# A transformer layer on one core: value projections grouped first, context steps queued behind units, and a layer norm cut into steps

## The chip, the core and the metric

The kernel runs on one core of one Trainium2 chip. The metric is the device time of one execution in microseconds (us), the median of three runs. TensorE (PE) multiplies matrices, VectorE (DVE), ScalarE (ACT) and GpSimd (POOL) work on vectors, and SyncE (SP) issues most of the DMA transfers. Each engine runs its own queue of instructions in order, and waits for other engines by semaphores.

## The reference

One post-norm decoder layer in float32, for x of 8 sequences of 100 tokens by 1024, and a context of 8 sequences of 722 tokens by 1024:

```
x = layernorm(x + retention(x))          # 8 heads, keys 128, values 256, gate; output projection Wo
x = layernorm(x + attention(x, context)) # 16 query heads, 4 key/value heads of 128
x = layernorm(x + ffn(x))                # silu(x w_gate) * (x w_up), then w_down, hidden 4096
```

The second line is where the change lies. Queries, keys and values of the tokens are q = x wq, k = x wk, v = x wv; q and k are RMS-normed and rotated. Keys and values of the context (k_ctx = context wk_ctx, normed, and v_ctx = context wv_ctx) are put in front of the tokens' own, and softmax(q k) v is projected by wo. The layer norm has no weights: (x - mean) / sqrt(var + eps).

## The kernel before

Everything is kept transposed, features on the 128 partitions and tokens in the columns, in two **halves** of four sequences (N = 400 columns). Products that are to have float32 accuracy are made of three matmuls on rounded parts: high by high (L90), high by low (L93), low by high (L94). The parts come from a *split* (L68): ACT casts to the rounded type, DVE subtracts to get the rest. A **unit** is one output block of 128 features for one half: 8 blocks of k by 3 matmuls, 24 matmuls of 128x400, in one PSUM bank (`proj`). PSUM has three banks for accumulators ("a"), four others ("s"), and one ("v"). Weights are loaded in pieces of 512 KB into `wst` (3 buffers, L74), and split into `w` (4 buffers). Context weights were split once at the start, and are loaded as 1 MB straight into a `w` buffer (`load_ws`, L84, from `wcd`).

The order of the program's text is mostly the order of each queue, but a scheduler may move instructions: `pin` keeps one in its place, `tc.high_priority()` pulls instructions ahead, `tc.issue_after(i)` queues one behind another without a wait.

The stages that the change touches, in order of time:

- **First output projection and layer norm** ("ln1", 500 to 611 us of the span). `out_proj(half, ...)` makes the 8 blocks m of one half, each from 16 blocks of k (two weights of 512 KB), adds the residual (`rs`, L271 or L269) into y, and sums the rows (L295). The norm of a half is done while the next matmuls run: the function returns a dictionary `todo` of what the next stage has to call before its k-th matmul group (`between`). Half 0's norm (`whole`: mean L320, y less mean L322, squares L301 and their sums L306, variance L324, scaling L312, split into z, store into zd) is called at once in the first block of half 1. Half 1's norm is partly early (`norm_early`, mean of seven blocks, L335, L337, L301) and ends in the next stage (`norm_late`, L291, L346, L343, L348, then L127 to L135, L312 and the z splits).
- **Second projections** ("l2", 587 to 850). z1[0] and z1[1] are the normed halves. For each of four key/value heads there are six weights: four of queries (i = 0 to 3), one of keys (4), one of values (5). They are taken in groups: (0..3) and (4, 5) for head 0, (0, 1), (2, 3), (4, 5) for the others; in a group all its weights run on z1[0], then on z1[1]. A query or key unit is followed by work on all other engines: square (L691, ACT), sum over partitions (L140, POOL), rotation (L148, L149 on ACT, L150 to L152 on DVE), inverse root (L127 to L135), scaling (L696), split (L68) and store into qd or kd. A value unit is copied to `vt` (L160, ACT), turned by four PE transposes (L163), split into vs (L687, one buffer) and stored into vd (L688).
- **The first context** is read by `load_context(0)`, called ahead of the second group: eight loads into `cs` (L634) and eight splits into the "big" tiles. The keys of the first two context products are made between groups: `context_keys` (L638) loads a key weight, and its `step` (L647) runs one more unit on the context, 24 matmuls of 128x362 or 128x360.
- **Second output projection and layer norm** ("lnp2", 1640 to 1750), the same `out_proj`, with one y buffer instead of two. Behind it come the feed-forward units; the first runs on z2[0] and carries the end of half 1's norm, and the next need half 1 as f and z.

The lines that order the second projections before the change:

```
for kv in range(NKV):
    for i0, i1 in ((0, 4), (4, 6)) if kv == 0 else ((0, 2), (2, 4), (4, 6)):
        if (kv, i0) == (0, 4):
            load_context(0)
        ws = [ws2.pop() if ws2 else load_w(w2[kv, i]) for i in range(i0, i1)]
        if (kv, i0) in ((1, 2), (2, 2)):
            step, kept = context_keys(kv - 1)
        if (kv, i0) in ((1, 2), (2, 0), (2, 2), (3, 0)):
            step(i0 == 0)
```

Of the kernel before, what the change touches and what calls it, by code (L numbers as in the profile page):

```python
# [16 lines left out]
P = 128  # L17
B, T, D = 8, 100, 1024
NB = 4
# [21 lines left out]
def decoder_layer(ctx, tc, xT, cT, w1, wo1, w2, wo2, wc, w3, wd, gw, qw, kw, trig, dec, mask, out):  # L41
# [12 lines left out]
    def bank(tag):  # L54
        return ps.tile([P, 512], F32, tag=tag, name=tag, bufs=banks[tag])

    def f32(ap):
        return ap.bitcast(F32)
# [4 lines left out]
    def split(dst, src):  # L63

        return split2(dst[:, 0], dst[:, 1], src)
# [4 lines left out]
    def load_w(src, w=None, pinned=None):  # L70
        st = wp.tile([P, KT * P], F32, tag="wst", name="wst", bufs=3)
        if w is None:
            w = wp.tile([P, 2, KT * P], FR, tag="w", name="w", bufs=4)
        nc.sync.dma_start(out=st, in_=src)  # L74
        if pinned:
            with tc.issue_after(pinned[0].ins), tc.issue_after(pinned[1].ins):
                split(w, st)
        else:
            split(w, st)
        return w  # L80
# [151 lines left out]
        return dcy  # L232


    def out_proj(half, w, load_o, res, yp, ybufs, p, make_z, dst, z, todo=None):


        og = load_o(half)
        y = None
        s1 = p.tile([P, N], F32, tag="s1", name="s1", bufs=2)  # L240
        early = {}
        first = 4 if half == 0 else 1
        for ms in [range(first)] + [[m] for m in range(first, KT)]:
            accs = [bank(("aaasaaaa", "sssaaass")[half][m])[:, :N] for m in ms]
            if half == 1 and KT - 1 in ms:
                todo = {QT: lambda: early.update(norm_early(y, s1, p))}
            for c in range(2):
                for m, acc in zip(ms, accs):
                    if half == 1 and m < 3:
                        with tc.high_priority():  # L250
                            wt = load_w(w[m, c])
                    else:
                        wt = load_w(w[m, c])
                    for k in range(KT):
                        kt = c * KT + k
                        pinned = between(todo, k) if c == 0 and m == ms[0] else False
                        rh, rl = og(kt)
                        a = acc if len(rh.shape) == 2 else bt(acc)
                        mmw(a, wt, k, rh, rl, kt == 0, kt == 2 * KT - 1, pinned)
            todo = None  # L260
            if y is None:
                y = yp.tile([P, KT, N], F32, tag="y", name="y", bufs=ybufs)
            for m, acc in zip(ms, accs):
                rs = yp.tile([P, N], F32, tag="rs", name="rs", bufs=2)
                nc.sync.dma_start(out=rs, in_=res[half, :, m])
                if early:
                    nc.vector.tensor_tensor(rs, rs, early["mean"], ALU.subtract)
                    with tc.high_priority():
                        nc.vector.tensor_tensor(y[:, m], acc, rs, ALU.add)  # L269
                else:  # L270
                    nc.vector.tensor_tensor(y[:, m], acc, rs, ALU.add)  # L271
                    add_up(s1, y, m)

        def whole():
            z.append(make_z(half))
            scaled(y, norm_root(y, s1, p), lambda m: dst[half, :, m], z[half])

        def late():
            norm_late(y, early, p)
            z.append(make_z(half))  # L280
            scaled(y, inv_root(p, early["vs"], eps_ln), lambda m: dst[half, :, m], z[half])

        if half == 0:
            return {QT: whole}, y
        sq = squares(y, p, [KT - 1])
        return {QT: lambda: summed(early["delta"], y[:, KT - 1], True, True),
                KT - 1: lambda: (summed(early["var"], early["sq"], True), summed(early["var"], sq, False, True), late())}, y
# [6 lines left out]
        if m > 0:  # L294
            nc.vector.tensor_tensor(s1, y[:, 0] if m == 1 else s1, y[:, m], ALU.add)  # L295

    def squares(y, p, ms):
        s2 = None
        for m in ms:
            sq = p.tile([P, y.shape[2]], F32, tag="sq", name="sq", bufs=2)  # L300
            nc.scalar.activation(sq, y[:, m], AF.Square)  # L301
            if s2 is None:
                s2 = sq
            else:
                s3 = p.tile([P, y.shape[2]], F32, tag="s2", name="s2", bufs=2)
                nc.vector.tensor_tensor(s3, s2, sq, ALU.add)  # L306
                s2 = s3
        return s2

    def scaled(y, r, dst, z=None):  # L310
        for m in range(KT):
            nc.vector.scalar_tensor_tensor(y[:, m], y[:, m], -0.5, r, ALU.mult, ALU.mult)  # L312
            if z is not None:
                split(z[m // QT][:, :, m % QT], y[:, m])
            nc.sync.dma_start(out=dst(m), in_=y[:, m])
# [294 lines left out]
    z1p = z1pool.__enter__()  # L610

    with sbuf("ln1", 1) as p:
        z1, todo = [], None
        for half in range(2):
            todo, _ = out_proj(half, wo1, load_o1, xT, p, 2, p, lambda _: [
                z1p.tile([P, 2, QT, N], FR, tag="z", name="z") for _ in range(2)], zd, z1, todo)
        ws2 = [load_w(w2[0, 0])]
        acc2 = [proj(ws2[0], z1[0], todo=todo)]


# [1 line left out]
    ka = kapool.__enter__()  # L622
    cz = []

    def load_context(b):

        cz.clear()
        for hf in range(2):
            n = SN[hf]
            z = [big([P, 2, QT, SH]) for _ in range(2)]  # L630
            for k in range(0, KT, 2):
                cs = wp.tile([P, KT * P], F32, tag="wst", name="cs", bufs=3)
                cs = cs[:, :2 * n].rearrange("p (k n) -> p k n", k=2)
                nc.sync.dma_start(out=cs, in_=cT[b, :, k:k + 2, hf * SH:hf * SH + n])  # L634
                split(z[k // QT][:, :, k % QT:k % QT + 2, :n], cs)
            cz.append(z)

    def context_keys(kv):  # L638

# [25 lines left out]
        return vt  # L665


    early = []
    with sbuf("l2", 2) as p:
        for kv in range(NKV):  # L670
            for i0, i1 in ((0, 4), (4, 6)) if kv == 0 else ((0, 2), (2, 4), (4, 6)):
                if (kv, i0) == (0, 4):
                    load_context(0)
                ws = [ws2.pop() if ws2 else load_w(w2[kv, i]) for i in range(i0, i1)]
                if (kv, i0) in ((1, 2), (2, 2)):
                    step, kept = context_keys(kv - 1)
                    early.append(kept)
                if (kv, i0) in ((1, 2), (2, 0), (2, 2), (3, 0)):
                    step(i0 == 0)
                for half in range(2):  # L680
                    bs = slice(half * NB, (half + 1) * NB)
                    for i in range(i0, i1):
                        acc = acc2.pop() if acc2 else proj(ws[i - i0], z1[half])
                        if i == 5:
                            tr = tokens_first(p, acc).rearrange("p (b d) -> p b d", b=NB)
                            vs = p.tile([T, NB, 2, P], FR, tag="vs", name="vs", bufs=1)
                            split2(vs[:, :, 0], vs[:, :, 1], tr)  # L687
                            nc.sync.dma_start(out=f32(vd[kv, :, bs]), in_=f32(vs))  # L688
                            continue
                        sq = p.tile([P, N], F32, tag="sq", name="sq")  # L690
                        nc.scalar.activation(sq, acc, AF.Square)  # L691
                        ss = all_red(p, sq, "ss")
                        tb = tq if i < 4 else tk
                        t = rope(p, acc, tb[:, 0], tb[:, 1], swapped=bank("s")[:, :N])
                        r = inv_root(p, ss, eps_k, at=bank("s")[:, :N])
                        nc.vector.scalar_tensor_tensor(  # L696
                            t, t, -0.5 if i < 4 else -0.5 * math.sqrt(P), r, ALU.mult, ALU.mult)
                        d = p.tile([P, NB, 2, T], FR, tag="d", name="d", bufs=3)
                        split2(d[:, :, 0], d[:, :, 1], bt(t))
                        nc.sync.dma_start(out=f32(qd[kv, i, :, bs] if i < 4 else kd[kv, :, bs]), in_=f32(d))  # L700
    z1pool.__exit__(None, None, None)


# [155 lines left out]


    with sbuf("lnp2", 1) as p:
        z2, todo = [], None
        for half in range(2):
            todo, y = out_proj(half, wo2, load_o2, zd, y2p, 1, p, make_z2, zd2, z2, todo)
        w0 = load_w(w3[0, 0])
        acc3 = [proj(w0, z2[0], tag=acc_tag(), todo=todo)]
        mixed2(y)
# [337 lines left out]
```

## Time and profile before

| | us |
|---|---|
| median of three runs | 2504.05 (2503.03 to 2505.15) |
| the profiled execution | 2504.06 |
| its span | 2502.3 |
| PE busy | 2463.2 |
| DVE busy | 1954.5 |
| ACT busy | 1343.0 |
| POOL busy | 464.8 |

The profile is of one execution. "Span" runs from the first to the last instruction; 1.76 us lie around it. Times in the text are us from the span's start. In a row of the profile, `L90 PE MATMUL a<-z,w` is the instruction of line 90 on PE that writes a tile named a from tiles z and w. A matmul's own duration (0.34 us) is longer than the distance to the next (0.181), since they overlap. "Granted clock" is the share of PE's full clock that was granted. DMA rows are transfers, and SPq rows are the issues of transfers on SP.

### The profile page before, as it was taken

Reading aid. Unit: us, or ns where it says so; the run is one execution under the profiler, and the core shown is the slowest. Engines: PE = TensorE matmul, PEld = TensorE weight load, DVE = VectorE, ACT = ScalarE, POOL = GpSimd, SP = SyncE. Lnnn points to the kernel's source line nnn. Section 1 sums busy time; section 2 is a strip of 40 time slices with the busy share of each in tenths; the row PEclk is TensorE's granted clock in tenths of the full one; section 3 lists DMA queues with packets and bytes.
Section 4 is the critical chain, followed back from the end, with each engine's and each line's share of the span. In section 5 each row is a group of like instructions: output and inputs, shape, how many; then the busy total and the mean of one; then the engine's idle time right before and its main releaser. Section 6 shows DMA issues by size and latency. Waiting matters only on the chain.

```text
span 2502.3 us, 37231 instructions
## 1 busy us (share of the span) xinstructions
PE 2463.2 (98%) x14068; PEld 2440.7 (98%) x14068; DVE 1954.5 (78%) x3101; ACT 1343.0 (54%) x2260; POOL 464.8 (19%) x234
## 2 busy tenths in 40 slices
PE   9999999997999999999999999999999999999997
PEld 9999999997999999999999999999999999999997
DVE  7778877567877688989999999866987777666756
ACT  6666676335767555656566666533544544432221
POOL 0111111002455343433433434100000000000000
PEclk9999999998999999999999999999999999999999
DMA  7333445774444654554554553574445444389731
GB/s 242 111 111 128 137 144 178 242 271 134 166 145 137 210 174 160 163 167 155 167 176 142 168 195 127 199 256 153 143 175 195 169 166 168 124 285 324 276 103 53
DMA packets 224451, 433.98 MB, mean 173 GB/s; under 512 B 47338, under 2 KB 168042, under 8 KB 211854
## 3 DMA queue, kind: packets, MB, share of 16 engines
q1 hardware_dynamic: 222542, 426.87, 50.2%
q0 software_dynamic: 1152, 4.19, 1.1%
q8 instruction: 111, 1.82, 0.3%
q14 instruction: 70, 0.57, 0.1%
q10 hardware_dynamic: 576, 0.52, 0.1%
HBM read 322.18 MB, written 109.35 MB: 172 GB/s over the span
## 4 chain that ended last, share of the span: by engine, by line
PE 93%; DVE 3%; DMA 2%; ACT 1%; issue 1%; POOL 0%; SPq 0%; DVEq 0%; ACTq 0%
PE a L94 20%; PE a L90 20%; PE a L93 20%; PE s L94 9%; PE s L93 9%; PE s L90 9%; PE v L94 2%; PE v L90 2%; PE v L93 2%; PE s L531 1%; PE s L734 1%; PE s L163 1%; DVE w L68 1%; DMA big<-o1d 1%; DVE y L312 0%
## 5 line engine op out<-in xcount | busy, mean ns | idle before, releaser
L90 PE MATMUL a<-big,w 128*128 128x400 f32 (+2 forms) x1808 | 609.5, 338 | 2.8 <-DMA w<-wcd 1.0
L93 PE MATMUL a<-big,w 128*128 128x400 f32 (+2 forms) x1808 | 609.3, 337 | 0.3 <-DVE big L68 0.3
L94 PE MATMUL a<-big,w 128*128 128x400 f32 (+2 forms) x1808 | 607.6, 337 | 0.4 <-DVE w L68 0.4
L68 ACT CAST w<-wst 128x1024 fp32r<-128x1024 f32 (+1 forms) x231 | 239.6, 1039 | 397.4 <-PE a L94 144.0
L68 DVE TENSOR_TENSOR w<-wst,w 128x1024 fp32r<-128x1024 f32 (+1 forms) x231 | 284.6, 1232 | 143.0 <-ACT w L68 141.7
L90 PEld LDWEIGHTS a<-big,w 128*128 128x128 f32 x1808 | 339.7, 188 | 5.9 <-ACT big L68 1.7
L93 PEld LDWEIGHTS a<-big,w 128*128 128x128 f32 x1808 | 340.3, 188 | 1.9 <-DVE big L68 1.0
L94 PEld LDWEIGHTS a<-big,w 128*128 128x128 f32 x1808 | 340.2, 188 | 1.2 <-DVE w L68 0.6
L90 PE MATMUL a<-z,w 128*128 128x400 f32 x680 | 236.4, 348 | 17.7 <-DVE t L150 16.0
L94 PE MATMUL a<-z,w 128*128 128x400 f32 x680 | 236.1, 348 | 0.0
L93 PE MATMUL a<-z,w 128*128 128x400 f32 x680 | 236.0, 347 | 0.0
L90 PE MATMUL s<-big,w 128*128 128x400 f32 x664 | 231.7, 349 | 2.4 <-ACT w L68 1.8
L94 PE MATMUL s<-big,w 128*128 128x400 f32 x664 | 229.9, 347 | 1.0 <-DVE w L68 1.0
L93 PE MATMUL s<-big,w 128*128 128x400 f32 x664 | 229.8, 346 | 0.0
L140 POOL PARTITION_ALL_REDUCE ss<-sq x56 | 150.7, 2693 | 328.8 <-DMA zd<-y 167.8
L651 POOL PARTITION_ALL_REDUCE kss<-ksq x64 | 166.7, 2604 | 127.8 <-ACT ksq L650 127.2
L90 PEld LDWEIGHTS a<-z,w 128*128 128x128 f32 x680 | 128.7, 189 | 19.5 <-DVE t L150 13.3
L768 ACT ACTIVATE s<-s,rk 128x400 f32<-128x400 f32 x160 | 87.9, 592 | 95.4 <-DVE sm L788 65.4
L90 PEld LDWEIGHTS s<-big,w 128*128 128x128 f32 x664 | 125.0, 188 | 5.3 <-ACT w L68 3.0
L94 PEld LDWEIGHTS a<-z,w 128*128 128x128 f32 x680 | 129.4, 190 | 0.0
L93 PEld LDWEIGHTS a<-z,w 128*128 128x128 f32 x680 | 128.7, 189 | 0.5
L94 PEld LDWEIGHTS s<-big,w 128*128 128x128 f32 x664 | 125.7, 189 | 1.7 <-DVE w L68 1.7
(356 smaller groups left out, 5443.8 us busy)
## 6 DMA issues: line engine op xcount, KB each, us to landing
wst<-in_w SPq DMA_DIRECT2D x135, 512.0 KB
w<-wcd SPq DMA_DIRECT2D x64, 1024.0 KB
wst<-in_wo SPq DMA_DIRECT2D x64, 512.0 KB
hd<-h SPq DMA_DIRECT2D x12, 1400.0 KB
wst<-in_wd SPq DMA_DIRECT2D x64, 256.0 KB
big<-o1d SPq DMA_DIRECT2D x16, 800.0 KB
qd<-d SPq DMA_DIRECT2D x32, 400.0 KB
q<-qd SPq DMA_DIRECT2D x32, 400.0 KB
```

The source lines that it names most:

```text
L68: return nc.scalar.copy(hi, src), nc.vector.tensor_tensor(lo, src, f32(hi), ALU.subtract)
L90: i = nc.tensor.matmul(acc, lh, rh, start=start, stop=False, skip_group_check=chain)
L93: nc.tensor.matmul(acc, lh, rl, start=False, stop=False, skip_group_check=chain)
L94: nc.tensor.matmul(acc, ll, rh, start=False, stop=stop, skip_group_check=chain)
L140: nc.gpsimd.partition_all_reduce(y, x, P, op)
L163: nc.tensor.transpose(tr[0:T, b * P:(b + 1) * P], vt[:, b * T:(b + 1) * T], ident)
L531: nc.tensor.matmul(bt(o)[:, b], vv[:, b * P:(b + 1) * P], pf[:, b], start=True, stop=True)
L651: nc.gpsimd.partition_all_reduce(ss[:, at], sq[:, at], P, RED.add)
L734: nc.tensor.transpose(tr[0:rows, (c - c0) * P:(c - c0 + 1) * P], vt[:, c * P:c * P + rows], ident)
L768: nc.scalar.activation(sc, sp, AF.Copy, scale=rk[:, c:c + 1])
```

## The change

Three things are done.

**Second projections.** The groups are now: the values of all four heads first, then for each head (0, 1) and (2, 3, 4). The first weight loaded is that of head 0's values. Context steps of keys come ahead of groups 2, 3, 5 and 7.

**The first context's steps.** `load_context` becomes a generator, `context_steps`; one of its eight load-and-split steps is taken ahead of each of the units 4 to 11, into buffers of its own (two), and both halves of its split are queued behind the split of the unit before (`tc.issue_after`).

**The norm of half 0.** In both output projections it is called in four steps: mean in block m = 0 of half 1, y less mean and squares of the first four blocks in m = 1, of the last four in m = 2, variance and the rest in m = 4. The inverse root reads the variance from PSUM without a copy. The weights of the first three blocks of half 1 are no longer loaded at high priority.

```diff
@@ out_proj
-            if half == 1 and KT - 1 in ms:
+            todo = steps.get(ms[0])
+            if half == 1 and KT - 1 in ms:
...
-                    if half == 1 and m < 3:
-                        with tc.high_priority():
-                            wt = load_w(w[m, c])
-                    else:
-                        wt = load_w(w[m, c])
+                    wt = load_w(w[m, c])
...
+        def centre():
+            kept["mean"] = bank("s")[:, :N]
+            pin(nc.tensor.matmul(kept["mean"], onem, s1, start=True, stop=True))
+        def less(ms):
+            for m in ms:
+                nc.vector.tensor_tensor(y[:, m], y[:, m], kept["mean"], ALU.subtract)
+            kept["sq"] = squares(y, p, ms, kept.get("sq"))
         def whole():
+            var = bank("v")[:, :N]
+            pin(nc.tensor.matmul(var, onem, kept["sq"], start=True, stop=True))
             z.append(make_z(half))
-            scaled(y, norm_root(y, s1, p), lambda m: dst[half, :, m], z[half])
+            scaled(y, inv_root(p, var, eps_ln), lambda m: dst[half, :, m], z[half])
...
-            return {QT: whole}, y
+            return {0: {QT: centre}, 1: {QT: lambda: less(range(QT))}, 2: {QT: lambda: less(range(QT, KT))},
+                    4: {QT: whole}}, y
@@ context_steps
-                cs = wp.tile([P, KT * P], F32, tag="wst", name="cs", bufs=3)
+                cs = pool.tile([P, KT * P if behind is None else 2 * SH], F32, tag="wst", name="cs", bufs=bufs)
...
-                split(z[k // QT][:, :, k % QT:k % QT + 2, :n], cs)
+                if behind is None:
+                    split(to, cs)
+                else:
+                    with tc.issue_after(behind[0].ins), tc.issue_after(behind[1].ins):
+                        split(to, cs)
...
+                yield
@@ second projections
+    groups = [[(kv, 5) for kv in range(NKV)]]
+    for kv in range(NKV):
+        groups += [[(kv, i) for i in range(2)], [(kv, i) for i in range(2, 5)]]
...
+        ctx0 = context_steps(0, p, 2, behind)
+        for g, group in enumerate(groups):
+            ws = [ws2.pop() if ws2 else load_w(w2[kv, i]) for kv, i in group]
+            if g in (2, 5):
+                step, kept = context_keys(len(early))
+                early.append(kept)
+            if g in (2, 3, 5, 7):
+                step(g in (3, 7))
...
+                    if 4 <= unit < 12:
+                        next(ctx0)
+                    acc = acc2.pop() if acc2 else proj(w, z1[half])
+                    unit += 1
...
+                        behind[:] = split2(vs[:, :, 0], vs[:, :, 1], tr)
...
+                    behind[:] = split2(d[:, :, 0], d[:, :, 1], bt(t))
```

More of the change, by code (lines that the diff above doesn't have):

```diff
@@ L232, in load_constants, with out_proj @@
         return dcy
-    def out_proj(half, w, load_o, res, yp, ybufs, p, make_z, dst, z, todo=None):
+    def out_proj(half, w, load_o, res, yp, ybufs, p, make_z, dst, z, steps={}):
         og = load_o(half)
@@ L259, in out_proj @@
                         mmw(a, wt, k, rh, rl, kt == 0, kt == 2 * KT - 1, pinned)
-            todo = None
             if y is None:
@@ L272, in out_proj @@
                     add_up(s1, y, m)
+        kept = {}
+        def centre():
[5 more added lines that the diff above has]
+            kept["sq"] = squares(y, p, ms, kept.get("sq"))
         def whole():
+            var = bank("v")[:, :N]
+            pin(nc.tensor.matmul(var, onem, kept["sq"], start=True, stop=True))
             z.append(make_z(half))
-            scaled(y, norm_root(y, s1, p), lambda m: dst[half, :, m], z[half])
+            scaled(y, inv_root(p, var, eps_ln), lambda m: dst[half, :, m], z[half])
         def late():
@@ L295, in add_up, with squares @@
             nc.vector.tensor_tensor(s1, y[:, 0] if m == 1 else s1, y[:, m], ALU.add)
-    def squares(y, p, ms):
-        s2 = None
+    def squares(y, p, ms, s2=None):
         for m in ms:
@@ L612, in decoder_layer @@
     with sbuf("ln1", 1) as p:
-        z1, todo = [], None
+        z1, todo = [], {}
         for half in range(2):
@@ L616, in decoder_layer @@
                 z1p.tile([P, 2, QT, N], FR, tag="z", name="z") for _ in range(2)], zd, z1, todo)
-        ws2 = [load_w(w2[0, 0])]
+        ws2 = [load_w(w2[0, 5])]
         acc2 = [proj(ws2[0], z1[0], todo=todo)]
@@ L623, in decoder_layer, with context_steps @@
     cz = []
-    def load_context(b):
+    def context_steps(b, pool, bufs, behind=None):
         cz.clear()
@@ L631, in load_context @@
             for k in range(0, KT, 2):
-                cs = wp.tile([P, KT * P], F32, tag="wst", name="cs", bufs=3)
+                cs = pool.tile([P, KT * P if behind is None else 2 * SH], F32, tag="wst", name="cs", bufs=bufs)
                 cs = cs[:, :2 * n].rearrange("p (k n) -> p k n", k=2)
                 nc.sync.dma_start(out=cs, in_=cT[b, :, k:k + 2, hf * SH:hf * SH + n])
-                split(z[k // QT][:, :, k % QT:k % QT + 2, :n], cs)
-            cz.append(z)
+                to = z[k // QT][:, :, k % QT:k % QT + 2, :n]
+                if behind is None:
[3 more added lines that the diff above has]
+                        split(to, cs)
+                if k == 0:
+                    cz.append(z)
+                yield
+    def load_context(b):
+        for _ in context_steps(b, wp, 3):
+            pass
     def context_keys(kv):
@@ L668, in decoder_layer @@
     early = []
-    with sbuf("l2", 2) as p:
[L670 to L700, printed above, removed]
@@ new lines, in decoder_layer @@
+    behind = [None, None]
+    groups = [[(kv, 5) for kv in range(NKV)]]
+    for kv in range(NKV):
+        groups += [[(kv, i) for i in range(2)], [(kv, i) for i in range(2, 5)]]
+    unit = 0
+    with sbuf("l2", 2) as p:
+        ctx0 = context_steps(0, p, 2, behind)
[6 more added lines that the diff above has]
+                step(g in (3, 7))
+            for half in range(2):
+                bs = slice(half * NB, (half + 1) * NB)
+                for (kv, i), w in zip(group, ws):
+                    if 4 <= unit < 12:
+                        next(ctx0)
+                    acc = acc2.pop() if acc2 else proj(w, z1[half])
+                    unit += 1
+                    if i == 5:
+                        tr = tokens_first(p, acc).rearrange("p (b d) -> p b d", b=NB)
+                        vs = p.tile([T, NB, 2, P], FR, tag="vs", name="vs", bufs=1)
+                        behind[:] = split2(vs[:, :, 0], vs[:, :, 1], tr)
+                        nc.sync.dma_start(out=f32(vd[kv, :, bs]), in_=f32(vs))
+                        continue
+                    sq = p.tile([P, N], F32, tag="sq", name="sq")
+                    nc.scalar.activation(sq, acc, AF.Square)
+                    ss = all_red(p, sq, "ss")
+                    tb = tq if i < 4 else tk
+                    t = rope(p, acc, tb[:, 0], tb[:, 1], swapped=bank("s")[:, :N])
+                    r = inv_root(p, ss, eps_k, at=bank("s")[:, :N])
+                    nc.vector.scalar_tensor_tensor(
+                        t, t, -0.5 if i < 4 else -0.5 * math.sqrt(P), r, ALU.mult, ALU.mult)
+                    d = p.tile([P, NB, 2, T], FR, tag="d", name="d", bufs=3)
+                    behind[:] = split2(d[:, :, 0], d[:, :, 1], bt(t))
+                    nc.sync.dma_start(out=f32(qd[kv, i, :, bs] if i < 4 else kd[kv, :, bs]), in_=f32(d))
@@ L861, in decoder_layer @@
     with sbuf("lnp2", 1) as p:
-        z2, todo = [], None
+        z2, todo = [], {}
         for half in range(2):
```

## The prediction

> **What bounds the kernel now.** I read the busy shares first, then PE's row of the 40 slices, then the waits of PE, then the stretches around each wait, two microseconds at a time.
>
> ```profile
> PE 2463.2 (98%) x14068; PEld 2440.7 (98%) x14068; DVE 1954.5 (78%) x3101; ACT 1343.0 (54%) x2260; POOL 464.8 (19%) x234
> ...
> PE   9999999997999999999999999999999999999997
> ```
>
> PE is busy for 98% of the span. So the end is the number of matmuls times their spacing, plus PE's holes and the slow clock behind them. The spacing is 0.181 us, 0.183 to 0.185 in the second half, so a unit of 24 matmuls lasts 4.36 to 4.4 us. Only one slice dips before the end, the tenth, and the waits of PE say who makes it:
>
> ```profile
> PE a L90 <- DVE t L150: 16.0, 2, 13.0
> PE s L90 <- ACT w L68: 1.8, 1, 1.8
> PE a L90 <- ACT d L68: 1.2, 1, 1.2
> ...
> PE a L90 <- DMA w<-wcd: 1.0, 2, 0.6
> ```
>
> (us in total, times, longest.) The first and third fall between 598 and 636 us, the second at 1663, the last at 678 and 740. The stretches add the clock after a stall (PE's busy time with its matmuls, granted clock third from the end):
>
> ```profile
> 598.00:612.00 14.00, 0.98 (x5) 0.65 (x4) 13.93 (x27) 8.05 (x16) 3.71 (x1) 0.65 0.69 246
> 612.00:614.00 2.00, 2.00 (x7) 1.98 (x7) 0.67 (x2) 0.39 (x1) 2.00 (x2) 0.50 0.00 0
> 614.00:616.00 2.00, 2.00 (x8) 1.98 (x7) 0.00 (x0) 1.93 (x5) 2.00 (x1) 0.54 0.00 0
> ...
> 636.00:638.00 2.00, 2.00 (x8) 1.97 (x8) 2.00 (x5) 1.89 (x5) 1.69 (x1) 0.58 0.95 371
> 638.00:640.00 2.00, 2.00 (x8) 1.97 (x8) 2.00 (x3) 0.68 (x2) 1.10 (x1) 0.56 0.37 143
> ...
> 1664.00:1666.00 2.00, 2.00 (x8) 2.00 (x7) 1.79 (x4) 0.95 (x3) 0.00 (x0) 0.50 1.02 399
> 1666.00:1668.00 2.00, 2.00 (x10) 2.00 (x9) 0.84 (x2) 0.16 (x1) 0.00 (x0) 0.71 1.03 401
> ```
>
> After 13.0 us idle the clock is 0.50 and 0.54 for 4 us: 1.9 us lost. After 3.0 idle it is 0.58 and 0.56: 1.7 lost. After 1.84 idle (1663) it is 0.50 and 0.71: 1.6 lost. I price a stall of 2 us or more at itself plus 1.7 to 1.9.
>
> **Part 1: all values first.** The 13.0 us: three "a" banks hold three q units, the fourth waits for L150, and L150 stands on DVE behind the whole norm of half 1:
>
> ```profile
> 597.94 0.91 DVE L68 TENSOR_TENSOR big<-cs,big 128x720 fp32r<-128x720 f32 x1 [0.88 <-ACT big L68]
> 598.77 0.57 DVE L348 TENSOR_TENSOR vs<-v,vs 128x400 f32<-128x400 f32 x1
> ...
> 603.26 3.97 DVE L312 SCALAR_TENSOR_TENSOR y<-y,r 128x400 f32<-128x400 f32 x8
> 607.15 3.97 DVE L68 TENSOR_TENSOR z<-y,z 128x400 fp32r<-128x400 f32 x8
> 611.03 0.57 DVE L150 TENSOR_TENSOR t<-a,tq 128x400 f32<-128x400 f32 x1
> ```
>
> The variance matmuls ran at 596.04 and 597.08, yet L348 waited for a context split. In this stage before loses 13.0 + 3.0 + 1.2 idle and 1.9 + 1.7 of clock: 20.8 us.
>
> In the changed kernel's instruction order the four first value units on z1[0] need no DVE, and no context split stands in the norm. But the transposes of the first value unit stand on PE three units later, and the copy to vt that they wait for stands on ACT behind the eight z casts, so behind the norm still. The variance pair stands 11 matmuls earlier: 596.04 - 11 x 0.181 = 594.05. What follows such a pair I take from the same chain in the second projection, where no context split stands in it: the pair starts at 1739.86, L348 1.54 us later (1741.40), and the last of the eight casts (L68 on ACT, 1745.71 to 1749.64) ends 8.24 us after that. Plus vt (0.49, L160) and a hand-over of 0.1: transposes at 594.05 + 1.54 + 8.24 + 0.59 = 604.4. PE reaches them at 594.05 + 1.35 (the pair) + 17 x 0.181 = 598.5. So a stall of **5.9** remains, with 1.9 of clock: 7.8 us. Behind it the chain vt, transposes (0.60), vs cast (0.59), vs split (0.69), store (some 2.5) takes about 4.4 us a unit against PE's 4.96, so I see no further stall there. Gain 20.8 - 7.8 = **13.0**.
>
> **Part 2: the context's steps behind units.** Their 8 DVE splits (0.82 spacing) and casts (0.80) now lie beside units 4 to 11; work, not PE time, and the buffers are ready long before the first key step. I cost them at nothing; the cover is PE's 4.4 us a unit against DVE's 3.5 (seven operations at 0.5) + 0.8 + half a weight split, and it lacks about 0.5 us in four units only.
>
> **Part 3: the regrouping moves the key weights.** Of the four w buffers, the first wk load (L84, 1 MB) gets in the new order the one that unit 11 frees, and the context step that needs it is the very next thing on PE. Before there was a unit between:
>
> ```profile
> 673.44 0.32 SPq L84 DMA_DIRECT2D w<-wcd  x1
> ...
> 678.34 0.40 PE L90 MATMUL a<-big,w 128*128 128x362 f32 x1 [0.56 <-DMA w<-wcd]
> ```
>
> Issue to use is 4.90 us, of which one unit hid all but 0.56. Now all of it shows. It also stands on SP behind a context load and a 512 KB weight load that is released in the last microsecond; the queue moved 398 GB/s at 676 to 678, so sharing could add 1.3. Ends 4.9 and 6.2, I take 5.5, in the middle since the release times of the two nearly coincide; with 1.7 of clock 7.2, less the 0.56 of before: **-6.6**. The second such load (group 5) keeps one unit of cover, as before.
>
> The Trainium skill, "DMA: Bandwidth & Descriptors", section "Anatomy of one DMA", gives about 2.0 us fixed plus bytes at 436 GB/s, measured for another queue kind: an estimate from the page of 4.4 us for 1 MB, so the load cannot hide in less than a unit. By it the term would be -5.5.
>
> **Part 4: the norm of half 0 in steps (both output projections).** At 1663 PE waited 1.84 us for a w cast that stands on ACT behind four squares; in the new order the matmul that needs it comes 12 matmuls (2.2 us) later, because weights of m below 3 are no longer pulled ahead. The cast keeps its place. So the stall goes, with its clock: 1.84 + 1.6 = **+3.4**. The same edit at 510 to 525, where about 1.1 us is idle: two o1d loads now stand ahead of a weight load on SP; bounds -1.5 and +1.0, I take 0. The variance of half 0 moves to m = 4, so scaling, z splits and stores come some 20 us later; half 1's first y add waits for the stores in the second projection (one y buffer) until about 1706 (before 1689). The row sums are then ready near 1717.5, ahead of the mean matmul at 1723: no stall, 6 us of cover.
>
> But at the end of that stage the order of matmuls turned: between the variance pair of half 1 and the first matmul on f there were 49 matmuls, now 15.
>
> ```profile
> 1741.40 0.57 DVE L348 TENSOR_TENSOR vs<-v,vs 128x400 f32<-128x400 f32 x1 [2.79 <-PE v L291]
> ...
> 1745.71 1.99 ACT L68 CAST f<-y 128x400 fp32r<-128x400 f32 x4 [1.92 <-DVE y L312]
> 1749.47 2.03 DVE L68 TENSOR_TENSOR f<-y,f 128x400 fp32r<-128x400 f32 x4
> ```
>
> From L348 to the first low half of f (1749.47 + 0.57) is 8.64 us. Before, 49 matmuls covered it (49 x 0.183 = 9.0; PE came to f at 1750.12). Now 18 matmuls do (3 use high halves alone): 3.3 us. Stall 8.64 + 0.1 - 3.3 = **5.4**, in two pieces, plus 1.8 of clock: **-7.2**.
>
> The Trainium skill, "TensorE: Matmul & The Clock Gate", section "What's actually happening", has the clock fall only after an idle window of about 3.4 us. The 1.84 us stall of this trace was followed by 0.50, so I follow the row; by the page part 4 would read +1.8 and -5.4, the same net within 0.2.
>
> **Sum.** 13.0 - 6.6 + 3.4 - 7.2 = 2.6 us less than the profiled execution's 2504.06 (span 2502.3 and 1.76 around it; the median is 2504.05): **2501.5**. A measurement of this kernel tells apart about 0.2%, 5.0 us: the forecast is "no change", between 2499.05 and 2509.05.
>
> **Rivals.**
> - A, faster: one of the two new stalls does not come, because DVE or ACT work lags so that PE's own units run late, or because the low half of f comes sooner once the norm's queue is free. The price is 6.6 or 7.2: 2494.3 to 2494.9. For it: PE is the only bound, and each is one wait. Against it: both are read from orders that are fixed. Both gone, 2488, I give little.
> - B, slower: q and k units in a row make DVE the bound. A unit costs DVE 3.5 us and half a weight split, and PE 4.36. The split takes 1.23 alone, but up to 2.46 in the trace while an all-reduce runs. At 1.72 per split they are level; that is the point. At 2.1 each unit is 0.2 over; over the 36 q and k units behind the first four this is 7 us, with two restarts of the clock about 10: 2511.5. For it: DVE was 10.00 of 10 us busy at 700 to 710. Against it: PE did not stop there, and eight context steps of 4 us give slack.
> - C, it doesn't do what it says: the value units bunch behind vt, vs (one buffer) and its store, so PE waits in each of the units 2 to 7 by, say, 1 us. The gain falls to 7: 2507.5, still within.
>
> **Numbers.** Forecast with C and the bounds of parts 3 and 4 (2499 to 2508): 0.44. A 0.30, of it 0.04 with both gone. B 0.26. The range reaches to A's and most of B's times: 2493 to 2511. Faster by over 0.2% 0.30, within 0.46, slower 0.24 (B partly within).
>
> **What would show it.** Step 1: the wait of the vt transposes near 604, about 6 us, and no wait for L150 of 13. Step 3: a wait for w<-wcd of about 5 near 645. Step 4: none at the start of the second projection, and two waits for f at its end, 2 and 3 us. Wrong would be: waits for t L150 spread over 650 to 850 (B), or either new wait under 2 us (A).

## The result, and the profile after

The changed kernel takes **2513.11 us** (median of 5 runs, 2512.07 to 2516.17) against 2504.05 in the same comparison: the ratio is 1.0039, with a 95% interval of 1.0028 to 1.0049. It is slower by 9 us, outside the range that was given. The profiled execution is the one of 2512.07 us; its span is 2510.3, so 8.0 us longer than the span before.

The first lines to look at are again the busy shares and PE's row of the 40 slices.

```profile
PE 2465.6 (98%) x14068; PEld 2445.1 (97%) x14068; DVE 1949.1 (78%) x3101; ACT 1341.2 (53%) x2258; POOL 465.9 (19%) x234
...
PE   9999999999899999999999999999999999999997
```

PE does the same 14068 matmuls and its row is still full. The dip has moved one slice to the right and is smaller. So the question is again which holes PE has. These are the waits of PE (us in total, times, longest):

```profile
PE a L90 <- DVE t L150: 11.6, 1, 11.6
PE s L163 <- ACT vt L160: 5.6, 1, 5.6
PE a L90 <- ACT s L130: 2.6, 1, 2.6
PE s L93 <- DVE f L68: 2.4, 1, 2.4
PE s L90 <- ACT f L68: 2.2, 1, 2.2
PE s L90 <- DVE s L793: 2.1, 1, 2.1
```

The stall of 13.0 is gone; the one of 5.6 at the first value unit's transposes is what remains of it. The two waits for f at the end of the second projection are there, as the prediction had them. The wait for the w cast at 1663 is gone. But the second projections now hold one stall of 11.6 at 648 to 659, where 5.5 was expected, and two more that were not expected at all: 2.6 at 740 and 2.1 at 859.

The clock after each stall comes from the stretches (width, PE, PEld, DVE, ACT and POOL busy, granted clock, DMA share, GB/s):

```profile
604.00:606.00 2.00, 2.00 (x7) 1.99 (x7) 2.00 (x4) 0.64 (x2) 0.00 (x0) 0.50 0.97 333
...
660.00:662.00 2.00, 2.00 (x9) 2.00 (x8) 2.00 (x5) 1.02 (x2) 0.00 (x0) 0.50 0.01 4
662.00:664.00 2.00, 2.00 (x8) 2.00 (x7) 1.41 (x3) 0.53 (x1) 0.00 (x0) 0.50 0.51 205
664.00:666.00 2.00, 2.00 (x10) 2.00 (x10) 0.23 (x1) 0.00 (x0) 0.00 (x0) 0.69 0.46 179
```

Each long stall is followed by some 4 to 5 us at about half clock: PE is "busy" for all of each stretch, but does 7 to 10 matmuls in 2 us where it does 13 or more at full clock. Counting (1 - clock) x PE's busy time, the stall of 5.6 costs 2.4 on top of itself, that of 11.6 costs 2.9, that of 2.6 costs 1.7, and the pair at f 2.0.

| place | before: idle + clock | after: idle + clock | gain, us |
|---|---|---|---|
| values first (598 to 636) | 17.2 + 3.6 | 5.6 + 2.4 | +12.8 |
| first key weight | 0.56 | 11.6 + 2.9 | -13.9 |
| second key weight | 0.46 | 2.6 + 1.7 | -3.8 |
| start of the second projection (1663) | 1.84 + 1.6 | none | +3.4 |
| 500 to 540 (two stretches of 20 us) | 1.1 | none | +1.1 |
| end of the second projection, f | none | 4.6 + 2.0 | -6.6 |
| start of the attention (859) | none | 2.1, clock stays 1.00 | -2.1 |
| sum | | | -9.1 |

The table is of the two profiled executions, whose spans differ by 8.0 us; it counts 1.1 too many. That it equals the difference of the medians, 9.1, is chance.

### The stall of 11.6, followed by hand

The first line of the waits names DVE's t (L150) as the releaser. This is the matmul in the PE timeline, with its idle time and the named releaser in brackets:

```profile
659.39 0.64 PE L90 MATMUL a<-big,w 128*128 128x362 f32 x1 [11.62 <-DVE t L150]
```

It reads big and w: it is the first step of the first context's keys, and it needs the 1 MB key weight. PE asked for it at 659.39 - 11.62 = 647.77. The SP queue's timeline shows when that weight was asked for:

```profile
649.44 0.34 SPq L729 DMA_DIRECT2D qd<-d  x1
650.26 0.37 SPq L644 DMA_DIRECT2D cs<-in_cT  x1
652.94 0.34 SPq L74 DMA_DIRECT2D wst<-in_w  x1
653.33 0.42 SPq L84 DMA_DIRECT2D w<-wcd  x1
```

The key weight (L84) is issued at 653.33, 5.56 us after PE needed it, and PE starts 6.06 us after the issue. Just ahead of it stands a 512 KB load into wst (L74). That load waits for its buffer, which a weight split frees; its two halves on ACT and DVE end at 650.90 and 652.92:

```profile
649.86 1.04 ACT L68 CAST w<-wst 128x1024 fp32r<-128x1024 f32 x1
```

```profile
650.94 1.98 DVE L68 TENSOR_TENSOR w<-wst,w 128x1024 fp32r<-128x1024 f32 x1 [0.23 <-ACT w L68]
```

So the key weight, whose own buffer came free when unit 11 ended, queued on SP behind a load that waited for a late split. The split was late because ACT, which does things in order, had been late all the way from the first value unit. The chain of waits in this stretch says why (start, us, what):

```profile
630.28 4.05 DMA vd<-vs
634.41 0.59 ACT vs L68
635.03 0.70 DVE vs L68
635.75 4.14 DMA vd<-vs
```

There is one vs buffer. From the fourth on, each value unit's cast into it (ACT) waits until the previous unit's values have landed in DRAM, and then come the cast, DVE's half and the next store: 0.59 + 0.70 + 4.1 and hand-overs, so 5.4 to 5.6 us a unit from 634 on and 6.2 to 6.6 before (the two earlier stores took 5.19 and 4.79). PE does a value unit in 4.96. In the profile's chain over 600 to 665, which it follows back through t, the vd store has 34% of the time, more than PE.

The stall of 2.6 stands at the same step of the second key weight (SP's timeline, then PE's):

```profile
734.93 0.33 SPq L74 DMA_DIRECT2D wst<-in_w  x1
735.42 0.32 SPq L729 DMA_DIRECT2D qd<-d  x1
735.86 0.36 SPq L84 DMA_DIRECT2D w<-wcd  x1
```

```profile
742.76 0.40 PE L90 MATMUL a<-big,w 128*128 128x362 f32 x1 [2.56 <-ACT s L130]
```

### The profile page after: what moved, and what is told of

Its sections match the earlier page's. It is cut to its first block, busy times and chain, and to the rows that moved or that the text cites. A ratio compares the mean times of both kernels' runs of the same rounds, so it can differ in the third digit from the quotient of the medians.

```text
span 2510.3 us, 37231 instructions
## 1 busy us (share of the span) xinstructions
PE 2465.6 (98%) x14068; PEld 2445.1 (97%) x14068; DVE 1949.1 (78%) x3101; ACT 1341.2 (53%) x2258; POOL 465.9 (19%) x234
## 4 chain that ended last, share of the span: by engine, by line
PE 91%; DMA 4%; DVE 3%; ACT 1%; issue 1%; SPq 0%; DVEq 0%; ACTq 0%
PE a L94 19%; PE a L90 19%; PE a L93 19%; PE s L94 9%; PE s L93 9%; PE s L90 9%; PE v L94 2%; PE v L90 2%; PE v L93 2%; PE s L541 1%; DMA vd<-vs 1%; PE s L763 1%; DMA tp<-in_xT 1%; PE s L163 1%; DVE y L322 1%
## 5 line engine op out<-in xcount | busy, mean ns | idle before, releaser
L90 PE MATMUL a<-big,w 128*128 128x400 f32 (+2 forms) x1808 | 611.6, 339 | 15.8 <-DVE t L150 11.6
```

The source lines that it names most:

```text
L90: i = nc.tensor.matmul(acc, lh, rh, start=start, stop=False, skip_group_check=chain)
```

## The experiments

The theory was: the stall of 11.6 is the landing of the key weight, made late by the one vs buffer. The rival was the profile's own word: DVE is late with t. Every ratio below is to the kernel before, run on the same chip, with its 95% interval. The experiments ran on different chips, where the kernel before took 2503.3 to 2503.9 us, so differences between two of them are good to about 1 us.

### A second vs buffer

```diff
-                        vs = p.tile([T, NB, 2, P], FR, tag="vs", name="vs", bufs=1)
+                        vs = p.tile([T, NB, 2, P], FR, tag="vs", name="vs", bufs=2)
```

> The changed kernel with two vs buffers instead of one; nothing else. Theory S (the store of the values): with one vs buffer each value unit's cast on ACT waits until the store before has landed (issue to landing 4.1 us, so 5.5 us a unit against PE's 5.0); ACT and DVE come late to the first query units, the split of the weight that SP's queue stands behind is late, and the key weight is issued 5.5 us after PE asked for it. Without that wait the stall of 11.6 us at the first context step falls to 5 to 7 (the load alone), and the time to 2506 to 2508. Rival D (DVE is overloaded by context splits beside the first query units, as the profile's releaser t L150 says): the stall stays at 9 to 11.6, the time at 2511 to 2513.

Measured: 2511.56 us, 1.0032 (1.0021 to 1.0042). The time is not what the theory gave: it lies in the rival's range, though the stall is shorter than the rival's 9 to 11.6. Still the trace speaks for the first half of the theory. The PE timeline and then SP's:

```profile
655.16 0.64 PE L90 MATMUL a<-big,w 128*128 128x362 f32 x1 [8.10 <-DMA w<-wcd]
```

```profile
646.17 0.34 SPq L74 DMA_DIRECT2D wst<-in_w  x1
647.09 0.34 SPq L84 DMA_DIRECT2D w<-wcd  x1
```

The weight is now issued at 647.09, just as PE comes to it (655.16 - 8.10 = 647.06), and the profile names it as the releaser. ACT's casts into vs, which no longer wait for the store, now start 4.8 us apart (614.79, 619.61, 624.42, 629.24). So "issued too late" was indeed the work of the one vs buffer. But the load itself now takes 8.1 us (8.07), not 5.5: a 512 KB load is issued 0.9 us ahead of it, a query store 0.4 and a context load 0.9 us behind it. So 3.5 us of the stall went, and 1.4 us of the clock behind it. In the profiled executions 1.4 us came back at the second key weight (2.7 idle and 3.0 of clock) and 1.4 at f (5.2 and 2.9), so the time fell by less than 2 us. The late issue alone was not the loss.

### The key weight one group earlier

```diff
-            if g in (2, 5):
+            if g in (1, 4):
                 step, kept = context_keys(len(early))
```

> The changed kernel with the key weight of each context asked for one group earlier (groups 1 and 4), so that it gets a w buffer that the values have freed; the context steps stay where they are. Theory S: what ends the 11.6 us is the landing of the key weight, so that wait goes; what is left is the lag of DVE, one or two waits for t L150 of 1 to 4 us together behind the step. The wait of 2.6 us before the third step goes too. Time 2503 to 2506. Rival D (the wait is for t L150 itself): 11.6 stays, only the 2.6 goes, 2510 to 2511.

Measured: 2499.18 us, 0.9982 (0.9973 to 0.9991), about 14 us less than the changed kernel. Nothing in DVE's work was taken away, only the place of the two key loads. The waits of PE:

```profile
PE s L163 <- ACT vt L160: 5.6, 1, 5.6
...
PE a L90 <- DVE t L150: 2.3, 1, 2.3
```

Both key stalls are gone (11.6 and 2.6). Of the waits that name t one of 2.3 is left, and it stands behind the step, at the next unit. The first matmul of the step now runs without a wait, between two of the L150 (DVE's timeline, then PE's):

```profile
644.73 0.56 DVE L150 TENSOR_TENSOR t<-a,tq 128x400 f32<-128x400 f32 x1
...
651.57 0.56 DVE L150 TENSOR_TENSOR t<-a,tq 128x400 f32<-128x400 f32 x1
```

```profile
645.70 0.33 PE L90 MATMUL a<-big,w 128*128 128x362 f32 x1
```

These are the second and third L150 of the query units, so the step needs at most the second. In the changed kernel that one ran long before the step began at 659.39:

```profile
647.88 0.57 DVE L150 TENSOR_TENSOR t<-a,tq 128x400 f32<-128x400 f32 x1
```

It ended at 648.45, 0.7 us after PE had begun to wait. So DVE's t was not the cause of the 11.6; the key weight was. The time is also lower than the theory's 2503 to 2506, whose sum is not on record; the two stalls with the clock behind them come to 18.8 us (14.5 and 4.3). The wait at the start of the attention grew, from 2.1 to 2.9 us, and now has 1.7 us of slow clock behind it.

### The two halves of the change alone

First the kernel before with the norm in steps (the changed `out_proj`, and nothing else; its last lines):

```diff
@@ out_proj of the kernel before
...
-            return {QT: whole}, y
+            return {0: {QT: centre}, 1: {QT: lambda: less(range(QT))}, 2: {QT: lambda: less(range(QT, KT))},
+                    4: {QT: whole}}, y
```

> The kernel before with only the norm of half 0 in steps (both output projections) and without the high priority of the weights. Theory: the 1.84 us wait at the start of the second norm goes with its clock (3.4 gained), and the two waits for f at its end come (2.2 and 2.4 with some 1.8 of clock, 6.4 lost): 2506 to 2508. Rival: the waits at the end belong to the regrouped projections and not to the norm: 2500 to 2501.

Measured: 2503.40 us, 0.9998 (0.9989 to 1.0007): no change. The waits of PE:

```profile
PE a L90 <- DVE t L150: 14.9, 3, 13.3
PE s L93 <- DVE f L68: 3.0, 1, 3.0
PE s L90 <- ACT f L68: 2.2, 1, 2.2
```

The two waits for f come with the norm in steps, as the theory said, and the one at 1663 goes (+3.4). The time is not the theory's 2506 to 2508. What it had not counted is the second projections' stage, whose code is untouched. There PE is idle 1.4 us less over 590 to 645, and the second wait for t (3.0 us before, at 633 to 636) has broken into two of 1.4 and 0.2 us, behind which the clock stays at 1.00, where before it fell to 0.66 over 635 to 640, which cost 1.7 us. The stall of 13.3 is followed by 2.6 us of slow clock, that of 13.0 before by 1.9, so 1.0 of the 1.7 is gained. With these 2.4, the 3.4 and the 1.1 at 500 to 540, 6.9 us are gained, and 8.1 lost at f (5.2 idle, 2.9 of clock); the account comes within 2 us of the measurement. Why the wait broke up is not shown.

Then the changed second projections with the old norm (the changed file, with the `out_proj` of the kernel before; its last lines):

```diff
@@ out_proj of the kernel after
...
-            return {0: {QT: centre}, 1: {QT: lambda: less(range(QT))}, 2: {QT: lambda: less(range(QT, KT))},
-                    4: {QT: whole}}, y
+            return {QT: whole}, y
```

> The kernel before with only the values first and the context's steps behind units; both norms as before. If the parts add up, this is the changed kernel less the norm's part: 2513.1 - 3.0 = 2510, with the 1.84 us wait at 1663 back and no wait for f. Rival: the parts do not add up, because the norm in steps makes room for the values (the first projection's first half), and this is slower than the changed kernel, 2514 or more.

Measured: 2510.68 us, 1.0025 (1.0014 to 1.0036). So the loss is in the second projections. The first line of its waits of PE:

```profile
PE a L90 <- DMA w<-wcd: 12.1, 1, 12.1
```

It is the same matmul in the same place as the 11.6 above, and here the profile calls it by the key weight. SP issues the weight 6.3 us before that matmul starts, 6.1 in the changed kernel. A wait for several things is put down to one of them; the name changed, not the cause.

### The variance one block earlier

The kernel with the earlier key weights, and in the second projection the variance of half 0 in block 3 of half 1 in place of 4. This puts back the 49 matmuls between half 1's variance and the first use of f.

```diff
-                    4: {QT: whole}}, y
+                    (3 if ybufs == 1 else 4): {QT: whole}}, y
```

> The kernel wk_one_group_earlier with one number changed: in the second projection the variance of half 0 comes in block m = 3 instead of 4. In its instruction order there are again 49 matmuls between the variance pair of half 1 and the first matmul on f, as in the kernel before (15 in the changed kernel). Theory C (the count of matmuls is the cover): both waits for f (2.2 and 3.0 us) go with some 1.8 us of slow clock, the rest stays: 2499.2 - 7.0 = 2492, to 2494. Rival: f is late since the norm in steps makes DVE late there; then the waits stay and the time is 2499.

Measured: 2491.11 us, 0.9952 (0.9940 to 0.9965): 8.1 us less than without the edit. Both waits for f are gone; with their clock they were 7.5 us, and 0.4 us of idle time is left in that stretch. The profiled executions differ by 10.8 us, of which 3.2 lie at the start of the attention (1.4 idle here, 2.9 with 1.7 of clock without the edit), which the edit does not touch.

The same edit on the kernel before with the norm in steps:

> The kernel norm_steps_alone with the variance of half 0 in block m = 3 instead of 4 in the second projection. Theory C again, without the regrouped projections: both waits for f go (2.2 and 3.0 us, with some 1.8 of clock), 2503.4 - 7.3 = 2496, to 2497. Rival: the gain seen behind the regrouped projections came from those; then 2500 to 2503.

Measured: 2496.01 us, 0.9972 (0.9961 to 0.9983), as expected. Both waits for f are gone here too, so the norm in steps, with the variance at the right block, gains 7 us without any of the new grouping.

### The context loads out of the key weight's way

With two vs buffers, the context's steps ahead of units 1 to 8 in place of 4 to 11, so that none of their loads runs beside the key weight:

```diff
-                    if 4 <= unit < 12:
+                    if 1 <= unit < 9:
                         next(ctx0)
```

> The kernel vs_two_buffers with the context's steps beside units 1 to 8 instead of 4 to 11, so that three of the four query units in front of the key step have no context split. The key weight stays where it is, issued when PE asks for it. Theory S2 (the load itself takes 8.0 us there, against 4.8 alone, because a weight, a context piece and query stores share the queues): the context pieces are away, so 8.1 falls to 6 to 7; 2509 to 2511. Rival D (DVE overloaded by context splits): with the splits away the stall falls to the bare 4.9 or less, 2506 to 2508. If nothing changes, neither the splits nor the pieces matter.

Measured: 2509.34 us, 1.0021 (1.0012 to 1.0030). The wait for the key weight falls from 8.1 to 6.4 us: the context loads beside it cost 1.7. It does not fall to the 4.9 of the kernel before. The 512 KB load 0.9 us in front and the query store 0.4 us behind are still there, and they may cost the rest; this was not tried. The wait at the start of the attention grew from 2.2 to 3.5.

### The first vt copy ahead of the norm's end

The kernel with the variance one block earlier; the first value unit's copy to vt (and its transposes) is called before the end of half 1's norm, so that it stands ahead of the eight z casts on ACT; and vs has two buffers.

```diff
-                KT - 1: lambda: (summed(early["var"], early["sq"], True), summed(early["var"], sq, False, True), late())}, y
+                KT - 1: lambda: (summed(early["var"], early["sq"], True), summed(early["var"], sq, False, True), late() if ybufs == 1 else None)}, y if ybufs == 1 else late
...
-            todo, _ = out_proj(half, wo1, load_o1, xT, p, 2, p, lambda _: [
+            todo, late1 = out_proj(half, wo1, load_o1, xT, p, 2, p, lambda _: [
...
         acc2 = [proj(ws2[0], z1[0], todo=todo)]
+        tr2 = [tokens_first(p, acc2[0])]
+        late1()
...
-                        tr = tokens_first(p, acc).rearrange("p (b d) -> p b d", b=NB)
-                        vs = p.tile([T, NB, 2, P], FR, tag="vs", name="vs", bufs=1)
+                        tr = (tr2.pop() if tr2 else tokens_first(p, acc)).rearrange("p (b d) -> p b d", b=NB)
+                        vs = p.tile([T, NB, 2, P], FR, tag="vs", name="vs", bufs=2)
```

> The kernel variance_one_block_earlier, with two vs buffers, and with the end of half 1's first norm called behind the vt copy of the first value unit, so that this copy stands ahead of the eight z casts on ACT. Theory: the 5.6 us wait of the transposes was only this place in ACT's queue; it falls to 1 to 2 us (the second unit's copy is still behind the casts), its 1.9 us of slow clock goes, and the 2.3 us wait for t L150 goes with the vs wait: 2483 to 2487. Rival: PE waits next for the normed half itself (z1[1], four value units later), and the stall comes back there: 2488 to 2491.

Measured: **2480.34 us, 0.9908 (0.9895 to 0.9922)**, faster than both kernels, by 23 and 33 us, and below the theory's 2483 to 2487. The first line of its waits of PE is the largest that is left:

```profile
PE s L163 <- ACT vt L160: 1.6, 1, 1.6
```

Against the kernel without the two edits, the transposes' stall falls from 5.6 with 1.8 of clock to 1.6 with none, the wait behind the key step (2.7 in all, with 1.5 of clock) is gone, and the one at the start of the attention falls from 1.4 to 0.2. Together that is 11.2 us; the medians differ by 10.8.

Then the same with one vs buffer, to see which of the two edits it was:

> The kernel vt_copy_ahead_vs_two with one vs buffer again, to part its two edits. Theory: the place of the vt copy is worth most of the 10.8 us between the two kernels (4.0 of stall and 1.9 of clock), the second buffer the rest, since the value units are now 6 us earlier and the one-buffer chain of 5.5 us a unit falls behind PE sooner: 2482 to 2486, with a wait for t L150 of 1 to 4 us. Rival: the second buffer does nothing once the key weight is early: 2480 to 2481.

Measured: 2488.96 us, 0.9948 (0.9934 to 0.9961). This is almost the 0.9952 without either edit, and 8.6 us above two buffers. The theory was wrong on the shares: it gave the place of the vt copy most of the gain. ACT's timeline, two value units in a row:

```profile
614.18 0.59 ACT L68 CAST vs<-s 100x512 fp32r<-100x512 f32 x1 [3.25 <-DMA vd<-vs]
...
620.24 0.59 ACT L68 CAST vs<-s 100x512 fp32r<-100x512 f32 x1 [4.13 <-DMA vd<-vs]
```

From the first such cast (601.22) to the eighth (642.15) it is 5.85 us a unit, and every one from the second on waits for the store. Removing the stall of 5.6 alone gains nearly nothing: PE comes earlier to a chain that runs at its own pace, and waits there instead (vt 4.5 us in four waits, then t and the attention's start). The same buffer was worth little in the changed kernel (2513.11 to 2511.56), where the key weight took over, and 8.6 us here. What it is worth by itself with the key weight early, without the vt copy ahead, was not run.

## Why the prediction was wrong

The picture of what bounds the kernel held: PE, its holes, and the clock behind them. Three of its four parts came out within 2 us. The sum (2.6 us gained forecast, 9.1 lost in the table) was missed by one wrong term, the first key weight (7.3 us), and by two that the sum does not hold, the second key weight (3.8) and the start of the attention (2.1).

- **Part 1, right in size, with a wrong sentence behind it.** The remaining stall was to be 5.9 us with 1.9 of clock, at 604.4; it is 5.6 with 2.4, at 602.5. PE came to the transposes 1.6 us earlier than worked out, and their input 1.9 earlier, so the two shifts cancel. Gain 12.8 for 13.0.
- **The step that failed is part 3's term of -6.6: "Ends 4.9 and 6.2, I take 5.5, in the middle since the release times of the two nearly coincide."** It measured -13.9. The load itself took 6.06 us from issue to use, inside those ends. But the release times did not coincide: the key weight's own buffer was free when PE came to the step, at 647.8, and the 512 KB load that stands in front of it on SP was released at 652.9, so the key weight was issued 5.56 us late. The clock behind the stall cost 2.9, for 1.7. Nor would 5.5 have held without the lateness: with two vs buffers the same load took 8.1 us, and 6.4 with the context loads away. Asking for the key weights one group earlier, and nothing else, took away both of their stalls and brought 2513.11 down to 2499.18.
- **What made the weight late is the step that part 1 ends on: "Behind it the chain vt, transposes (0.60), vs cast (0.59), vs split (0.69), store (some 2.5) takes about 4.4 us a unit against PE's 4.96, so I see no further stall there."** With vt's 0.49 its own numbers give 4.9. The store takes 4.0 to 5.2 us, for 400 KB on 100 partitions; no run shows 2.5 for it. The trace of before has 2.43 us for a store of 200 KB (zd<-y, at 605.81). And the chain was compared with PE alone. It closes through one buffer, so its true pace is cast, split, store: 5.4 to 6.6 us a unit. Rival C named this buffer and its store, and put its price into PE's units 2 to 7. It did not show there, because PE does not wait for vs; it came out some eight units later, through ACT's queue, the weight split and SP's queue, in the key weight.
- **"The second such load (group 5) keeps one unit of cover, as before" failed too.** It is issued 0.93 us behind a 512 KB load and 0.44 behind a query store, and PE starts 6.9 us after the issue. One unit covers 4.4: PE waits 2.56, and the clock falls to 0.50. That is 3.8 us. The wait goes when the weight is asked for earlier, and with two vs buffers the same wait (2.7) is named w<-wcd, so the name L130 is again not the cause.
- **The start of the attention (2.1) was not looked at.** Query and key units now run to the end of the stage, and the last key store is issued at 852.95, where before it was at 842.94. The link from that store to the wait is read from the trace and was not tried by itself. The order of the units alone does not make the wait: with the vt copy ahead and two vs buffers the order at the end is the same, and the wait there is 0.2 us.
- **Part 2, right but for the loads.** The eight context steps cost no PE time of their own. Their loads cost the key weight 1.7 us in the kernel with two vs buffers.
- **Part 4, right.** The 3.4 at the start came whole; the waits for f are 2.2 and 2.4 with 2.0 of clock, 6.6 in place of 7.2; and taking them away by one block gave 7 to 8 us twice. The 500 to 540 stretch gave 1.1, just past the bound of 1.0.
- **Rival B gave nearly the right time for a wrong reason.** Its 2511.5 was to come from DVE as the bound in the query and key units. DVE is indeed 10.00 of 10 us busy in several stretches from 690 on, but PE is full beside it, and moving the key loads alone won back 14 us.
- **Rival A did not happen**: none of the new stalls failed to come.

The Trainium skill, "TensorE: Matmul & The Clock Gate", section "What's actually happening", has the clock fall after one idle window of about 3.4 us, in a window that runs freely. The rows here differ, and they decide for this case. The clock does not go by the length of the stall alone: 1.84 us idle (1663, before) and 2.56 (740, after) were followed by 0.50, while 2.08 us idle (859, after) left it at 1.00:

```profile
744.00:746.00 2.00, 2.00 (x9) 2.00 (x8) 2.00 (x5) 1.64 (x4) 0.00 (x0) 0.50 0.80 131
...
862.00:864.00 2.00, 2.00 (x14) 2.00 (x13) 1.51 (x4) 1.55 (x3) 0.00 (x0) 1.00 0.88 242
```

Behind the same stall of 5.6 us at the first transposes, six kernels lost between 1.7 and 2.8 us of clock.

## What to carry to other kernels

When units are regrouped so that the same kind comes many times in a row, work out the pace of each loop that closes through a single buffer, with the landing of its store in it, and compare that with the unit on the bounding engine; an excess need not show where it arises, but comes out at the end of the in-order queues behind it. For a load that stops being covered, count from the time when the instruction in front of it on its queue can issue, not from the time when its own buffer is free. And a stall taken away in front of a slower chain gives nothing until the chain is widened: here two edits, taken one after the other, were worth 1 to 2 us and 8.6 us, and neither can be read from the first stall's length.

## What was not expected of the hardware

- The same 1 MB load took 4.9 us from issue to use in the kernel before, 6.1 with 512 KB issued just ahead of it, 6.9 with 512 KB and a store ahead, 6.4 with 512 KB ahead and a store behind, and 8.1 with a context load behind as well. The Trainium skill, "DMA: Bandwidth & Descriptors", section "Issuing engines are not separate DMA queues", says that all transfers run on the same 16 DMA engines and interleave, which agrees with these five numbers.
- A stall of about 2 us may or may not slow the clock: see the rows above. In one comparison (the norm in steps alone) a wait of 3.0 us that was followed by 1.7 us of slow clock had broken into two of 1.4 and 0.2 that were followed by none, in a stage whose code was the same.
- A wait with several causes changed its named releaser between two kernels (t in the one, w<-wcd in the other) at the same matmul with nearly the same length, 11.6 and 12.1 us. The t that the matmul can need had ended 10.9 us before it started.
